# Loads of x moved to GpSimd's queue, products made four ahead, and preparation's transfers reordered

## The chip, the cores and the metric

The kernel runs on one core of a Trainium2 chip. The metric is device time in microseconds (us) of one execution. The engines are TensorE (PE in the profile), VectorE (DVE), ScalarE (ACT), GpSimd (POOL) and SyncE (SP); SyncE, ScalarE and GpSimd also issue transfers (DMA), and these issues are shown as SPq, ACTq and POOLq.

## The reference

The input is x of shape (1024, 39, 64): 1024 rows b, 39 fields f, 64 embedding columns e. Three layers of a compressed interaction network follow, each a product of the layer's state with the input, mixed by a weight matrix:

```
def _cin_layer(Xk, X0, W, b):
    Wr = W.reshape(O, Hk, Fdim)
    return jnp.einsum('bhe,bfe,ohf->boe', Xk, X0, Wr) + b[None, :, None]

Xk = X0
for W, b in ((W0, b0), (W1, b1), (W2, b2)):
    Xk = _cin_layer(Xk, X0, W, b)
    outs.append(Xk.sum(axis=-1))
return concatenate(outs, axis=-1) @ fc_w.T + fc_b
```

The output has one number per row b. All values are float32.

## The kernel before, in words

The sum over e and the final weights allow the last two layers to be folded. Preparation folds W2 and W1 with fc_w into one table (`wide`, in device memory) and lays W0 out in another (`wide0`). The main matmul then takes, for each column (b, e), the products of pairs of fields and gives 128 rows: 64 that stand for the folded upper layers and 64 of the first layer. Products of fields are symmetric, so all pairs of the 39 fields are covered by seven chunks of 117 = 3 x 39 products: each chunk multiplies two tiles in which the fields are rotated by different distances.

The 65536 columns (b, e) are worked in NBLK = 32 blocks of BLK = 2048 columns. For one block n:

- `load(n)` brings x into `xs`, 39 partitions of 2048 columns, in rows of 64 numbers (256 bytes).
- `store(n)` writes `xs` twice, one copy under the other, into a scratch tensor `xd` in device memory (78 rows of 8 KB).
- `roll(n)` reads four tiles `r0` to `r3` of 117 rows from `xd`, each with its own rotation (936 KB each), and two thirds of a fifth tile, `q`, whose last third holds ones.
- `product(n, c)`, c = 0 to 6, multiplies two of these tiles on VectorE into `p`. The pairs in order are r0 r1, r0 r2, r1 r2, r0 r3, r1 r3, r2 r3, r0 q.
- `multiply(n, c, p)` runs four matmuls of 512 columns with the weights `wa[:, c]` and adds into the block's two accumulators `po` (each of 1024 columns).
- `fields(n)` copies `xs` on ScalarE into the lower rows of two tiles `g`.
- `finish(n)` works the accumulators off: ScalarE adds a bias (`x1`), VectorE multiplies it with the other half into `g` and sums over e into `sums`, twice per block.

Loads, stores and rolls are all issued on SyncE's queue. In block n it issues roll(n+1), then load(n+2), then store(n+2), which waits for that load. Buffers: three of `xs`, four of `xd`, two each of r0 to r3 and q, four of `p`, four accumulators, two each of `g` and `x1`. The order within each engine is that of the code (`manual_schedule`). Transfers issue in order on each queue and wait for the tiles that they read or overwrite.

Before the loop, SyncE loads W2, then block 0 of x, stores it, loads block 1 and issues roll(0). ScalarE loads the small weights and W1, later writes ten pieces (`part`) of the folded table to `wide`. GpSimd copies W0 four times into `wide0` and gathers from it the right half of `wa` and `wb`, row by row (117 rows of 256 bytes per gather). The left halves are gathered from `wide`: those of `wa` by ScalarE, those of `wb` by SyncE (lines 213 to 219). In block 0 VectorE adds `wb[:, c]` to `wa[:, c]` (line 284) before the first matmul of chunk c.

The lines of the loop that set the order:

```
for n in range(NBLK):
    if n + 1 < NBLK:
        roll(n + 1)
    if n + 2 < NBLK:
        load(n + 2)
        store(n + 2)
    for c in range(NCHUNK):
        p = product(n, c)
        if n == 0:
            nc.vector.tensor_tensor(wa[:, c], wa[:, c], wb[:, c], ALU.add)
        multiply(n, c, p)
        if n > 0 and c == 3:
            finish(n - 1)
    fields(n)
```

Lines named below: load L106, store L112 and L113, rolls L118 (r) and L120, L121 (q), wide0 copies L135, part writes L194, gathers L201 and L204, product L237, matmul L244, field copy L256, bias L263, the two steps of finish on VectorE L267 and L271, the add of the weights L284.

Of the kernel before, what the change touches and what calls it, by code (L numbers as in the profile page):

```python
# [48 lines left out]
PAIRS = ((0, 1), (0, 2), (1, 2), (0, 3), (1, 3), (2, 3))  # L49
NCHUNK = len(PAIRS) + 1  # L50
MM = 512
SUB = 1024
BLK = 2048
# [3 lines left out]
FW = 2 * F  # L57
# [21 lines left out]
def cin_kernel(ctx: ExitStack, tc: tile.TileContext, x, w0t, b0, w1, b1, w2, b2, fc_w, fc_b, out):  # L79
# [10 lines left out]
    work = ctx.enter_context(tc.tile_pool(name="work", bufs=2))  # L90
# [4 lines left out]
    q = []  # L95
    for i in range(2):
        qt = const.tile([K, BLK], F32, name=f"q{i}")
        nc.gpsimd.memset(qt, 1.0)  # L98
        q.append(qt)

    xv = x.rearrange("b f e -> f b e")
    xs, xd, r = {}, {}, {}

    def load(n):
        xs[n] = stage.tile([F, BLK], F32, name="xs", tag="xs")
        nc.sync.dma_start(  # L106
            xs[n].rearrange("p (b e) -> p b e", e=E), xv[:, n * BB : (n + 1) * BB, :]
        )

    def store(n):  # L110
        xd[n] = xds.tile([FW, BLK], F32, name="xd", tag="xd")
        nc.sync.dma_start(xd[n][0:F], xs[n])  # L112
        nc.sync.dma_start(xd[n][F:FW], xs[n])  # L113

    def roll(n):
        r[n] = [rolls.tile([K, BLK], F32, name=f"r{i}", tag=f"r{i}") for i in range(4)]
        for i in range(4):
            nc.sync.dma_start(r[n][i], rows(xd[n], BASE[i], [(1, F), (STEP[i], NG)], BLK))  # L118
        qt = q[n % 2]
        nc.sync.dma_start(qt[0:K:NG], xd[n][LAST : LAST + F])  # L120
        nc.sync.dma_start(qt[1:K:NG], xd[n][0:F])  # L121


    w2s = const.tile([H, FH], F32, name="w2s")
    nc.sync.dma_start(w2s, w2)
    fc = const.tile([H, 3], F32, name="fc")
    nc.scalar.dma_start(fc, fc_w.rearrange("o (l h) -> h (o l)", h=H))
    w1s = const.tile([H, FH], F32, name="w1s")
    nc.scalar.dma_start(w1s, w1)
    wide0 = dram.tile([FW * FW, H], F32, name="wide0")  # L130
    wide0v = wide0.rearrange("(b a) h -> b (a h)", a=FW)
    w0v = w0t.rearrange("b a h -> b (a h)")
    for i in range(2):
        for k in range(2):
            nc.gpsimd.dma_start(  # L135
                wide0v[i * F : (i + 1) * F, k * F * H : (k + 1) * F * H], w0v
            )
    bias = const.tile([H, 2], F32, name="bias")
    nc.scalar.dma_start(bias[:, 0:1], b1.rearrange("(h o) -> h o", o=1))
    nc.scalar.dma_start(bias[:, 1:2], b2.rearrange("(h o) -> h o", o=1))  # L140
    b0s = const.tile([128, 1], F32, name="b0s")
    nc.scalar.dma_start(b0s[H:128], b0.rearrange("(h o) -> h o", o=1))
    fcb = const.tile([1, 1], F32, name="fcb")
    nc.scalar.dma_start(fcb, fc_b.rearrange("(p o) -> p o", o=1))

    load(0)
    store(0)
    load(1)
    roll(0)

    wa = const.tile([K, NCHUNK, 2 * H], F32, name="wa")
    wb = const.tile([K, NCHUNK, 2 * H], F32, name="wb")
    nc.vector.memset(wa[:, NCHUNK - 1, :], 0.0)
    nc.vector.memset(wb[:, NCHUNK - 1, :], 0.0)
    wfin = const.tile([H + F, 1], F32, name="wfin")
    nc.vector.memset(wfin[0:H], 1.0)
    fc2 = const.tile([H, 32], F32, name="fc2")
    nc.vector.tensor_copy(fc2, fc[:, 2:3].to_broadcast([H, 32]))  # L158

    v2 = const.tile([H, FX], F32, name="v2")  # L160
    nc.vector.tensor_copy(v2[:, FW:FX], fc[:, 1:2].to_broadcast([H, 2]))


    n8 = 8 * F
    pv = psum.tile([128, 2, MM], F32, name="pv", tag="po")
    for half in range(2):
        for t in range(4):
            g = 4 * half + t
            nc.tensor.matmul(  # L169
                pv[32 * t : 32 * t + 32, half, 0:n8],  # L170
                fc2,
                w2s[:, g * n8 : (g + 1) * n8],
                start=True,
                stop=True,
            )
    vrow = const.tile([128, 2, n8], F32, name="vrow")
    for half in range(2):
        nc.vector.tensor_copy(vrow[:, half], pv[:, half, 0:n8])  # L178
        nc.scalar.dma_start(v2[32 * half : 32 * half + 32, 0:F], vrow[0:128:32, half])
    nc.vector.tensor_copy(v2[:, F:FW], v2[:, 0:F])  # L180


    w1v = w1s.rearrange("o (h f) -> o f h", f=F)
    wide = dram.tile([FX * FW, H], F32, name="wide")
    widev = wide.rearrange("(b a) h -> b (a h)", a=FW)
    for g in range(5):
        f0, f1 = 8 * g, min(8 * g + 8, F)
        n = (f1 - f0) * H
        pt = psum.tile([128, SUB], F32, name="pt", tag="po")
        nc.tensor.matmul(pt[0:FX, :n], v2, w1v[:, f0:f1, :], start=True, stop=True)  # L190
        part = const.tile([FX, MM], F32, name=f"part{g}")
        nc.vector.tensor_copy(part[:, :n], pt[0:FX, :n])  # L192
        for k in range(2):
            nc.scalar.dma_start(widev[:, (k * F + f0) * H : (k * F + f1) * H], part[:, :n])  # L194


    def gather(engine, dst, table, i, k, cols):

        first = BASE[k] * FW + BASE[i]
        steps = [(FW + 1, F), (STEP[k] * FW + STEP[i], NG)]  # L200
        engine.dma_start(dst[:, cols], rows(table, first, steps, H))  # L201
# [4 lines left out]
    tcol, wcol = slice(0, H), slice(H, 2 * H)  # L206
    for c, (i, k) in enumerate(PAIRS):
        gather(nc.gpsimd, wa[:, c], wide0, i, k, wcol)
        gather(nc.gpsimd, wb[:, c], wide0, k, i, wcol)
    line(nc.gpsimd, wa, wide0, 0, wcol, LAST * FW, FW + 1)  # L210
    line(nc.gpsimd, wb, wide0, 0, wcol, LAST, FW + 1)
    line(nc.gpsimd, wa, wide0, 1, wcol, 0, FW + 1)
    for c, (i, k) in enumerate(PAIRS):
        gather(nc.scalar, wa[:, c], wide, i, k, tcol)
        gather(nc.sync, wb[:, c], wide, k, i, tcol)
    line(nc.scalar, wa, wide, 0, tcol, LAST * FW, FW + 1)
    line(nc.sync, wb, wide, 0, tcol, LAST, FW + 1)
    line(nc.scalar, wa, wide, 1, tcol, 0, FW + 1)
    line(nc.sync, wa, wide, 2, tcol, FW * FW, 1)
    store(1)  # L220


# [5 lines left out]
    kfin = const.tile([1, 1], F32, name="kfin")  # L228
    nc.scalar.activation(kfin, pc[0:1, MM : MM + 1], AF.Identity, bias=fcb, scale=float(E))

    sums = const.tile([H + F, B], F32, name="sums")
    po, g = {}, {}

    def product(n, c):
        a, b = (r[n][PAIRS[c][0]], r[n][PAIRS[c][1]]) if c < len(PAIRS) else (r[n][0], q[n % 2])
        p = prods.tile([K, BLK], F32, name="p", tag="p")
        nc.vector.tensor_tensor(p, a, b, ALU.mult)  # L237
        return p

    def multiply(n, c, p):  # L240
        if c == 0:
            po[n] = [psum.tile([128, SUB], F32, name="po", tag="po") for _ in range(BLK // SUB)]
        for m in range(BLK // MM):
            nc.tensor.matmul(  # L244
                po[n][m // 2][:, bass.ts(m % 2, MM)],
                wa[:, c, :],
                p[:, bass.ts(m, MM)],
                start=(c == 0),
                stop=(c == NCHUNK - 1),
            )  # L250
# [21 lines left out]
                sums[:, b_at : b_at + SB], gt.rearrange("p (b e) -> p b e", e=E), AX.X, ALU.add  # L272
            )

    for n in range(NBLK):
        if n + 1 < NBLK:
            roll(n + 1)
        if n + 2 < NBLK:
            load(n + 2)
            store(n + 2)  # L280
        for c in range(NCHUNK):
            p = product(n, c)
            if n == 0:
                nc.vector.tensor_tensor(wa[:, c], wa[:, c], wb[:, c], ALU.add)  # L284
            multiply(n, c, p)
            if n > 0 and c == 3:
                finish(n - 1)
        fields(n)
    finish(NBLK - 1)

    y = const.tile([1, B], F32, name="y")
# [47 lines left out]
```

## Time and profile before

| what | value |
|---|---|
| time, median of 3 runs | 911.06 us (905.61 to 913.46) |
| the profiled execution | 906.01 us, span 904.2 us |
| TensorE matmuls busy | 808.2 us, 89% of the span |
| VectorE busy | 659.8 us, 73% |
| ScalarE busy | 140.8 us, 16% |
| GpSimd busy | 15.0 us, 2% |
| granted TensorE clock, mean | 0.985 |
| moved by transfers | 179.36 MB, 198 GB/s |

The profile is of one execution. The span runs from the first to the last instruction; 1.8 us of the execution's time lie outside it. A row of a group gives line, engine, operation, tiles written and read, shapes, count, then busy us, mean ns of one, and the idle time of the engine before these instructions with what ended most of it. A row in order of time gives start, duration, engine and operation, and in brackets the idle time before it and what ended it. A row of waits gives the total in us, how often, and the longest. The busy time of matmuls is modelled from their pipelining.

### The profile page before, as it was taken

The numbers are of one execution on the slowest core, as the hardware profiler recorded it, in microseconds if no ns is written. First come the engines' busy times: TensorE is split into PE (matmuls) and PEld (weight loads), VectorE is DVE, ScalarE is ACT, GpSimd is POOL, SyncE is SP. The second block draws the span as 40 slices with busy tenths as digits, with TensorE's granted clock in tenths as the row PEclk, the third lists the DMA queues.
The fourth block names the chain that finished last, engine by engine and source line by source line (L and its number), as shares of the span: only waits on it lengthen the run. The fifth ranks groups of instructions, "written<-read, shape, count | busy, mean of one in ns | idle before, by whom it ended". The sixth has DMA issues, their size and how long they took to land.

```text
span 904.2 us, 4982 instructions
## 1 busy us (share of the span) xinstructions
PE 808.2 (89%) x1828; PEld 344.5 (38%) x1828; DVE 659.8 (73%) x372; ACT 140.8 (16%) x133; POOL 15.0 (2%) x25
## 2 busy tenths in 40 slices
PE   1369999989989998999999998999989988998996
PEld 0024444434434433444344443433433333333432
DVE  0258888768968776888777786885867865778855
ACT  0001111110111111011111111011111110111112
POOL 4100000000000000000000000000000000000000
PEclk9999999999999999999999999999999999998999
DMA  8666676766667766666567766667675676766640
GB/s 190 199 226 205 176 233 229 229 167 187 211 186 240 215 229 190 225 227 217 163 218 215 240 237 179 190 173 190 236 229 176 165 179 214 230 159 191 221 149 0
DMA packets 67819, 179.36 MB, mean 198 GB/s; under 512 B 46548, under 2 KB 46747, under 8 KB 47544
## 3 DMA queue, kind: packets, MB, share of 16 engines
q1 hardware_dynamic: 64614, 174.66, 63.6%
q10 hardware_dynamic: 2446, 2.45, 1.1%
q0 software_dynamic: 736, 1.95, 0.7%
q8 instruction: 14, 0.23, 0.1%
q14 instruction: 9, 0.07, 0.0%
HBM read 156.98 MB, written 23.61 MB: 200 GB/s over the span
## 4 chain that ended last, share of the span: by engine, by line
DMA 79%; SPq 14%; PE 2%; DVE 2%; issue 2%; ACT 0%; ACTq 0%; DVEq 0%
DMA xs<-in_x 54%; DMA xd<-xs 20%; SPq L118 8%; SPq L120 3%; SPq L121 2%; DMA r<-xd 2%; DMA v<-vrow 1%; SPq L112 1%; PE pt L190 1%; DMA q<-xd 1%; PE po L244 1%; DVE p L237 1%; DMA fc<-in_fc_w 1%; DMA wide<-part 1%; DVE g L267 1%
## 5 line engine op out<-in xcount | busy, mean ns | idle before, releaser
L244 PE MATMUL po<-p,wa 117*128 117x512 f32 x1792 | 794.0, 603 | 70.8 <-DVE p L237 47.0
L237 DVE TENSOR_TENSOR p<-r,r 117x2048 f32<-117x2048 f32 x192 | 431.7, 2286 | 195.5 <-DMA r<-xd 173.7
L244 PEld LDWEIGHTS po<-p,wa 117*128 117x128 f32 x1792 | 341.2, 193 | 522.8 <-issue 429.6
L263 ACT ACTIVATE x<-po,b0s 64x1024 f32<-64x1024 f32 x64 | 71.1, 1110 | 385.4 <-PE po L244 385.4
L256 ACT COPY g<-xs 39x1024 f32<-39x1024 f32 x64 | 66.7, 1043 | 328.1 <-DVE sums L271 328.1
L267 DVE SCALAR_TENSOR_TENSOR g<-po,fc,x 64x1024 f32<-64x1024 f32 x64 | 81.2, 1269 | 5.7 <-ACT x L263 5.7
L271 DVE TENSOR_REDUCE sums<-g 103x16 f32<-103x1024 f32 x64 | 78.1, 1220 | 2.2
L237 DVE TENSOR_TENSOR p<-r,q 117x2048 f32<-117x2048 f32 x32 | 73.1, 2283 | 0.8 <-issue 0.8
L190 PE MATMUL pt<-w1s,v 64*80 64x512 f32 (+1 forms) x10 | 9.5, 1109 | 11.5 <-DVE v L180 11.5
L284 DVE TENSOR_TENSOR wa<-wa,wb 117x128 f32<-117x128 f32 x7 | 2.0, 285 | 10.0 <-DMA wb<-wide 10.0
L190 PEld LDWEIGHTS pt<-w1s,v 64*80 64x80 f32 x10 | 2.2, 228 | 18.3 <-DVE v L180 12.6
L169 PE MATMUL pv<-w2s,fc 64*32 64x312 f32 x16 | 2.3, 724 | 6.9 <-DVE fc L158 6.9
L192 DVE COPY part<-pt 80x512 f32<-80x512 f32 (+1 forms) x5 | 3.4, 674 | 6.8 <-PE pt L190 6.8
L227 ACT ACT_TABLE_LOAD x1 | 1.3, 1283 | 43.7 <-DMA wa<-wide 43.7
L180 DVE COPY v<-v 64x39 f32<-64x39 f32 x1 | 0.2, 176 | 10.4 <-DMA v<-vrow 10.4
L294 PE MATMUL py<-sums,wfin 103*1 103x512 f32 x4 | 2.0, 590 | 3.7 <-DVE sums L271 3.7
L201 POOL DMA_DIRECT2D wb<-wide x6 | 4.5, 744 | 0.0
L201 POOL DMA_DIRECT2D wa<-wide x6 | 4.2, 704 | 11.7 <-DMA wide<-in_w0t 11.6
L158 DVE COPY fc<-fc 64x32 f32<-64x32 f32 x1 | 0.2, 173 | 5.5 <-DMA fc<-in_fc_w 5.5
L98 POOL MEMSET q<- 117x2048 f32 x2 | 3.5, 1804 | 0.3 <-POOLq L326 0.3
L169 PEld LDWEIGHTS pv<-w2s,fc 64*32 64x32 f32 x16 | 0.6, 154 | 7.6 <-DVE fc L158 6.9
L178 DVE COPY vrow<-pv 128x312 f32<-128x312 f32 x2 | 0.9, 476 | 2.4 <-PE pv L169 2.4
(21 smaller groups left out, 8.2 us busy)
## 6 DMA issues: line engine op xcount, KB each, us to landing
r<-xd SPq DMA_DIRECT2D x128, 936.0 KB
xd<-xs SPq DMA_DIRECT2D x64, 312.0 KB
q<-xd SPq DMA_DIRECT2D x64, 312.0 KB
xs<-in_x SPq DMA_DIRECT2D x32, 312.0 KB
wide<-in_w0t POOLq DMA_DIRECT2D x4, 380.2 KB, 10.2
wide<-part ACTq DMA_DIRECT2D x8, 160.0 KB
w2s<-in_w SPq DMA_DIRECT2D x1, 624.0 KB
w1s<-in_w ACTq DMA_DIRECT2D x1, 624.0 KB
```

The lines of the kernel that those rows point to most:

```text
L112: nc.sync.dma_start(xd[n][0:F], xs[n])
L118: nc.sync.dma_start(r[n][i], rows(xd[n], BASE[i], [(1, F), (STEP[i], NG)], BLK))
L120: nc.sync.dma_start(qt[0:K:NG], xd[n][LAST : LAST + F])
L121: nc.sync.dma_start(qt[1:K:NG], xd[n][0:F])
L190: nc.tensor.matmul(pt[0:FX, :n], v2, w1v[:, f0:f1, :], start=True, stop=True)
L201: engine.dma_start(dst[:, cols], rows(table, first, steps, H))
L237: nc.vector.tensor_tensor(p, a, b, ALU.mult)
L244: nc.tensor.matmul(po[n][m // 2][:, bass.ts(m % 2, MM)], wa[:, c, :], p[:, bass.ts(m, MM)], start=(c == 0), stop=(c == NCHUNK - 1),)
L256: nc.scalar.copy(gt[H : H + F], xs[n][:, bass.ts(h, SUB)])
L263: nc.scalar.activation(t, po[n][h][H:128, :], AF.Identity, bias=b0s[H:128])
L267: nc.vector.scalar_tensor_tensor(gt[0:H], po[n][h][0:H, :], fc[:, 0:1], x1[h], ALU.add, ALU.mult)
L271: nc.vector.tensor_reduce(sums[:, b_at : b_at + SB], gt.rearrange("p (b e) -> p b e", e=E), AX.X, ALU.add)
```

## The change

The loads of blocks 1 and up are issued on GpSimd's queue, three blocks ahead of the block that TensorE works on; `xs` gets four buffers and `xd` five. The order on SyncE in block n is roll(n+1), store(n+2). Products are made four chunks ahead of the matmuls that use them, across the block's border; the finish of the block before, and the copies of fields, follow the first chunk's matmuls instead of the fourth's and the seventh's. In preparation two of the four `wide0` copies go from GpSimd to ScalarE, block 1 of x is loaded on GpSimd after its gathers together with block 2, q is filled with ones later on GpSimd, and the first four `wb` gathers from `wide` go from SyncE to ScalarE, each behind the `wa` gather of its chunk. Tiles that only preparation uses lie in a pool of their own, whose space `g` and `x1` take over. No arithmetic is changed.

The diff, cut to its core:

```diff
-    xds = ctx.enter_context(tc.tile_pool(name="xds", bufs=4, space=DRAM))
-    stage = ctx.enter_context(tc.tile_pool(name="stage", bufs=3))
+    xds = ctx.enter_context(tc.tile_pool(name="xds", bufs=5, space=DRAM))
+    stage = ctx.enter_context(tc.tile_pool(name="stage", bufs=4))
...
-    def load(n):
+    def load(n, engine):
         xs[n] = stage.tile([F, BLK], F32, name="xs", tag="xs")
-        nc.sync.dma_start(
+        engine.dma_start(
...
+        nc.sync.dma_start(w2s, w2)
+        nc.scalar.dma_start(fc, fc_w.rearrange("o (l h) -> h (o l)", h=H))
+        nc.scalar.dma_start(w1s, w1)
+        load(0, nc.sync)
+        for i in range(2):
+            for k in range(2):
+                engine = nc.scalar if i else nc.gpsimd
+                engine.dma_start(wide0v[i * F : (i + 1) * F, k * F * H : (k + 1) * F * H], w0v)
...
-    load(0)
-    store(0)
-    load(1)
-    roll(0)
+        store(0)
+        roll(0)
...
-    for c, (i, k) in enumerate(PAIRS):
-        gather(nc.scalar, wa[:, c], wide, i, k, tcol)
-        gather(nc.sync, wb[:, c], wide, k, i, tcol)
...
+    def gathers(engine, other, table, cols):
+        for c, (i, k) in enumerate(PAIRS):
+            gather(engine, wa[:, c], table, i, k, cols)
+            gather(engine if c < 4 else other, wb[:, c], table, k, i, cols)
+        line(engine, wa, table, 0, cols, LAST * FW, FW + 1)
+        line(other, wb, table, 0, cols, LAST, FW + 1)
+        line(engine, wa, table, 1, cols, 0, FW + 1)
+
+    gathers(nc.gpsimd, nc.gpsimd, wide0, slice(H, 2 * H))
+    load(1, nc.gpsimd)
+    load(2, nc.gpsimd)
+    gathers(nc.scalar, nc.sync, wide, slice(0, H))
+    line(nc.sync, wa, wide, 2, slice(0, H), FW * FW, 1)
     store(1)
...
+    AHEAD = 4
+    steps = [(n, c) for n in range(NBLK) for c in range(NCHUNK)]
+    p = {s: product(*s) for s in steps[:AHEAD]}
+    for at, (n, c) in enumerate(steps):
+        if c == 0:
+            if n + 1 < NBLK:
+                roll(n + 1)
+            if n + 2 < NBLK:
+                store(n + 2)
+            if n + 3 < NBLK:
+                load(n + 3, nc.gpsimd)
+        if n == 0:
+            nc.vector.tensor_tensor(wa[:, c], wa[:, c], wb[:, c], ALU.add)
+        multiply(n, c, p.pop((n, c)))
+        if c == 0:
+            if n > 0:
+                finish(n - 1)
+            fields(n)
+        if at + AHEAD < len(steps):
+            p[steps[at + AHEAD]] = product(*steps[at + AHEAD])
     finish(NBLK - 1)
```

More of the change, by code (lines that the diff above doesn't have):

```diff
@@ L130, in cin_kernel @@
+    bias = const.tile([H, 2], F32, name="bias")
+    b0s = const.tile([128, 1], F32, name="b0s")
+    fcb = const.tile([1, 1], F32, name="fcb")
+    wfin = const.tile([H + F, 1], F32, name="wfin")
+    kfin = const.tile([1, 1], F32, name="kfin")
+    q = [const.tile([K, BLK], F32, name=f"q{i}") for i in range(2)]
     wide0 = dram.tile([FW * FW, H], F32, name="wide0")
     wide0v = wide0.rearrange("(b a) h -> b (a h)", a=FW)
[L132 to L137, printed above, removed]
@@ L152, in cin_kernel @@
[L152 to L165, printed above, removed]
@@ L166, in cin_kernel @@
[L166 to L179, printed above, removed]
@@ L180, in cin_kernel @@
-    nc.vector.tensor_copy(v2[:, F:FW], v2[:, 0:F])
-    w1v = w1s.rearrange("o (h f) -> o f h", f=F)
     wide = dram.tile([FX * FW, H], F32, name="wide")
     widev = wide.rearrange("(b a) h -> b (a h)", a=FW)
[L186 to L194, printed above, removed]
+    prep = tc.tile_pool(name="prep", bufs=1)
@@ new lines, in cin_kernel @@
+    with prep as prep:
+        w2s = prep.tile([H, FH], F32, name="w2s")
+        w1s = prep.tile([H, FH], F32, name="w1s")
+        nc.sync.dma_start(w2s, w2)
+        nc.scalar.dma_start(fc, fc_w.rearrange("o (l h) -> h (o l)", h=H))
+        nc.scalar.dma_start(w1s, w1)
+        load(0, nc.sync)
+        w0v = w0t.rearrange("b a h -> b (a h)")
+        for i in range(2):
+            for k in range(2):
+                engine = nc.scalar if i else nc.gpsimd
+                engine.dma_start(wide0v[i * F : (i + 1) * F, k * F * H : (k + 1) * F * H], w0v)
+        nc.scalar.dma_start(bias[:, 0:1], b1.rearrange("(h o) -> h o", o=1))
+        nc.scalar.dma_start(bias[:, 1:2], b2.rearrange("(h o) -> h o", o=1))
+        nc.scalar.dma_start(b0s[H:128], b0.rearrange("(h o) -> h o", o=1))
+        nc.scalar.dma_start(fcb, fc_b.rearrange("(p o) -> p o", o=1))
+        for qt in q:
+            nc.gpsimd.memset(qt, 1.0)
+        store(0)
+        roll(0)
+        nc.vector.memset(wa[:, NCHUNK - 1, :], 0.0)
+        nc.vector.memset(wb[:, NCHUNK - 1, :], 0.0)
+        nc.vector.memset(wfin[0:H], 1.0)
+        nc.vector.tensor_copy(fc2, fc[:, 2:3].to_broadcast([H, 32]))
+        nc.vector.tensor_copy(v2[:, FW:FX], fc[:, 1:2].to_broadcast([H, 2]))
+        n8 = 8 * F
+        pv = psum.tile([128, 2, MM], F32, name="pv", tag="po")
+        vrow = prep.tile([128, 2, n8], F32, name="vrow")
+        for half in range(2):
+            for t in range(4):
+                g = 4 * half + t
+                nc.tensor.matmul(
+                    pv[32 * t : 32 * t + 32, half, 0:n8],
+                    fc2,
+                    w2s[:, g * n8 : (g + 1) * n8],
+                    start=True,
+                    stop=True,
+                )
+            nc.vector.tensor_copy(vrow[:, half], pv[:, half, 0:n8])
+            nc.scalar.dma_start(v2[32 * half : 32 * half + 32, 0:F], vrow[0:128:32, half])
+        nc.vector.tensor_copy(v2[:, F:FW], v2[:, 0:F])
+        w1v = w1s.rearrange("o (h f) -> o f h", f=F)
+        for g in range(5):
+            f0, f1 = 8 * g, min(8 * g + 8, F)
+            n = (f1 - f0) * H
+            pt = psum.tile([128, SUB], F32, name="pt", tag="po")
+            nc.tensor.matmul(pt[0:FX, :n], v2, w1v[:, f0:f1, :], start=True, stop=True)
+            part = prep.tile([FX, MM], F32, name=f"part{g}")
+            nc.vector.tensor_copy(part[:, :n], pt[0:FX, :n])
+            for k in range(2):
+                nc.scalar.dma_start(widev[:, (k * F + f0) * H : (k * F + f1) * H], part[:, :n])
@@ L273, in finish @@
             )
[L275 to L286, printed above, removed]
+    AHEAD = 4
[14 more added lines that the diff above has]
+            if n > 0:
                 finish(n - 1)
-        fields(n)
+            fields(n)
+        if at + AHEAD < len(steps):
+            p[steps[at + AHEAD]] = product(*steps[at + AHEAD])
     finish(NBLK - 1)
```

36 lines of the change are left out of this document (5 added, 31 removed).

## The prediction

> **What bounds the kernel now.** I read the page's first and fourth parts, then SyncE's waits, then one block of the loop in order of time. Busy shares first, as us, share of the span, instructions:
>
> ```profile
> PE 808.2 (89%) x1828; PEld 344.5 (38%) x1828; DVE 659.8 (73%) x372; ACT 140.8 (16%) x133; POOL 15.0 (2%) x25
> DMA xs<-in_x 54%; DMA xd<-xs 20%; SPq L118 8%; SPq L120 3%; SPq L121 2%; DMA r<-xd 2%; DMA v<-vrow 1%; SPq L112 1%; PE pt L190 1%; DMA q<-xd 1%; PE po L244 1%; DVE p L237 1%; DMA fc<-in_fc_w 1%; DMA wide<-part 1%; DVE g L267 1%
> SPq L112 <- DMA xs<-in_x: 480.0, 31, 19.3
> SPq L118 <- DMA xd<-xs: 134.6, 62, 3.8
> ```
>
> TensorE is busy for 89%, yet the chain that ended last runs through transfers and SyncE's queue: 54% is the landing of a load, 20% that of a store. SyncE itself waits for the load 31 times, 480.0 us (15.5 each). One block of SyncE's work, with the first and the last rolls of the loop around it, start and duration in us:
>
> ```profile
> 59.06 4.12 SPq L118 DMA_DIRECT2D r<-xd  x4
> ...
> 470.24 0.30 SPq L112 DMA_DIRECT2D xd<-xs  x1
> ...
> 475.10 3.88 SPq L118 DMA_DIRECT2D r<-xd  x4
> ...
> 480.59 0.56 SPq L106 DMA_DIRECT2D xs<-in_x  x1
> 496.77 0.31 SPq L112 DMA_DIRECT2D xd<-xs  x1
> ...
> 853.90 4.03 SPq L118 DMA_DIRECT2D r<-xd  x4
> ```
>
> Rolls, then the load (5.5 us later), its landing and the store (16.2 later), the store's landing and the next rolls (470.24 to 475.10: 4.86). Together 26.5 us. Over the span, 30 such periods lie between the rolls at 59.06 and those at 853.90: 26.49 us each. This ring is the bound. TensorE's own need is less:
>
> ```profile
> 58.90 0.19 PEld L244 LDWEIGHTS po<-p,wa 117*128 117x128 f32 x1 [0.24 <-issue]
> ...
> 74.78 0.19 PEld L244 LDWEIGHTS po<-p,wa 117*128 117x128 f32 x1 [0.24 <-issue]
> L244 PE MATMUL po<-p,wa 117*128 117x512 f32 x1792 | 794.0, 603 | 70.8 <-DVE p L237 47.0
> ```
>
> 37 matmul steps lie between the two weight loads, so one step is 0.429 us; a block has 1792/32 = 56, so 24.04 us, and 32 blocks 769.2 us. The row of all matmuls shows 794.0 busy (24.8 more) and 47.0 of waits for products.
>
> **The change, part by part.** *The load leaves SyncE's queue.* Its four-line ring loses the load and its wait; what remains is rolls, store, landing, rolls. What the transfers themselves need is read from windows of 2 us (length, busy PE, PEld, DVE, ACT, POOL, granted clock, transfer share, GB/s):
>
> ```profile
> 490.00:492.00 2.00, 2.00 (x6) 0.81 (x5) 2.00 (x2) 0.00 (x0) 0.00 (x0) 1.00 0.86 266
> 492.00:494.00 2.00, 2.00 (x6) 0.93 (x5) 2.00 (x2) 0.00 (x0) 0.00 (x0) 1.00 0.91 159
> 494.00:496.00 2.00, 2.00 (x6) 0.80 (x6) 2.00 (x2) 0.00 (x0) 0.00 (x0) 1.00 0.68 61
> 496.00:498.00 2.00, 2.00 (x6) 0.92 (x5) 1.97 (x3) 0.42 (x1) 0.00 (x0) 1.00 0.31 75
> ```
>
> The rate falls at about 492.5, where the roll's big rows end and the load's 256-byte rows begin: the rolls took 17.4 us from their issue, the load another 4.3 (to 496.77) at a high share for few bytes. The store now issues behind the rolls without waiting, so its issue and start are covered; I put 3.6 of its 4.86 us behind the rolls (estimate: the wait for landing, at most 3.8 in the row above). The transfer ring is then 17.4 + 3.6 = 21.0 us if the load runs wholly in gaps, 25.3 if it costs its 4.3 in full. With the store's latency uncovered too it is 17.4 + 4.86 + 4.3 = 26.5, nothing gained. I take half of the load, 23.1, since share 0.31 in the window at 496 shows a gap of a few us in each period but not one that fits the load whole. That is under TensorE's 24.04: **the bound passes to TensorE.**
>
> Does VectorE keep up?
>
> ```profile
> L237 DVE TENSOR_TENSOR p<-r,r 117x2048 f32<-117x2048 f32 x192 | 431.7, 2286 | 195.5 <-DMA r<-xd 173.7
> L267 DVE SCALAR_TENSOR_TENSOR g<-po,fc,x 64x1024 f32<-64x1024 f32 x64 | 81.2, 1269 | 5.7 <-ACT x L263 5.7
> L271 DVE TENSOR_REDUCE sums<-g 103x16 f32<-103x1024 f32 x64 | 78.1, 1220 | 2.2
> 484.86 2.29 DVE L237 TENSOR_TENSOR p<-r,r 117x2048 f32<-117x2048 f32 x1 [3.76 <-DMA r<-xd]
> 488.37 2.29 DVE L237 TENSOR_TENSOR p<-r,r 117x2048 f32<-117x2048 f32 x1 [1.22 <-DMA r<-xd]
> ```
>
> A block asks 7 x 2.286 + 2 x 1.269 + 2 x 1.220 = 21.0 us of it, under 24.04.
>
> *Products four ahead; finish after the first chunk.* No work is added. Product s+4 waits for the matmuls of chunk s (four buffers). Queued behind it on VectorE at a block's start T: the product for chunk 3 (to T+2.3), the finish of the block before (5.0, to T+7.3), the product for chunk 4 (to T+9.6), which TensorE wants at T+4x3.43 = T+13.7. So 4 us of cover; if the finish were late by more, TensorE would wait. The last product of a block ends at about T+14.2, and only then may the rolls two blocks on overwrite its tiles. They have 24 x 2 - 14 = 34 us until TensorE wants them; the first product starts 9.8 after the issue (475.10 to 484.86), the second 13.3 after, so 12 us suffice. The 47.0 us of product waits should nearly go; I keep 5 for rolls that run late (the longest load wait, 19.3 against 15.5, shows that transfers vary by some 4 us).
>
> *The slow clock.* Of the 24.8 us over 769.2, five steps at the start go at half pace (0.85 us from one weight load to the next), 5 x 0.43 = 2.2; the others come at and after waits, where the granted clock falls:
>
> ```profile
> 55.18 0.34 PEld L244 LDWEIGHTS po<-p,wa 117*128 117x128 f32 x1 [0.52 <-issue]
> 56.03 0.34 PEld L244 LDWEIGHTS po<-p,wa 117*128 117x128 f32 x1 [0.52 <-issue]
> ...
> 81.00:109.00 28.00, 28.00 (x66) 12.35 (x65) 24.42 (x14) 4.97 (x5) 0.00 (x0) 1.00 0.67 192
> 800.00:870.00 70.00, 65.31 (x145) 28.20 (x144) 50.37 (x27) 11.88 (x11) 0.00 (x0) 0.95 0.68 212
> ```
>
> Clock 1.00 where TensorE never pauses, 0.95 where it does. Without the waits I count this as gone, all but the 2.2.
>
> *Preparation reordered.* Now TensorE starts at 54.16:
>
> ```profile
> 18.00 0.33 SPq L106 DMA_DIRECT2D xs<-in_x  x1
> 28.59 14.87 SPq L118 DMA_DIRECT2D r<-xd  x4
> 36.83 0.89 ACTq L201
> 37.75 4.07 DMA wa<-wide
> 44.35 9.18 DMA q<-xd
> 45.19 7.08 SPq L201 DMA_DIRECT2D wb<-wide  x6
> 53.82 0.29 DVE L284 TENSOR_TENSOR wa<-wa,wb 117x128 f32<-117x128 f32 x1 [10.03 <-DMA wb<-wide]
> 54.16 21.20 PE L244 MATMUL po<-p,wa 117*128 117x512 f32 x44 [23.52 <-DMA wb<-wide]
> ```
>
> The last to come is the first wb gather: on SyncE behind the rolls, issued at 45.19 and landed by 53.82. It moves to ScalarE as the second gather, 36.83 + 0.89 + 0.89 + 4.07 = 42.7. But four products now precede the add on VectorE, so all four r tiles must have landed first. Lower bound of the start: 43. Upper: the fourth r landed before q (44.35 + 9.18 = 53.5), plus a product and the add: 56. The rolls' issue stretched over 14.87 us here and 3.88 in the loop, so waits on other transfers held them; if these stay, the start stays near the upper end. The first load of block 1 no longer stands ahead of the rolls (18.00), but two copies of wide0 join ScalarE's queue, and three loads, the two moved copies and the parts' writes share the transfers with the rolls. I take 47.5, nearer the gathers, whose row ended the wait. SyncE keeps 4 of its 8 gather issues, some 6 us less, so the rolls of block 1 go at 53 instead of 59; TensorE wants them at 47.5 + 2.2 + 24.0 = 73.7, 53 + 12 = 65 is in time.
>
> *GpSimd.* It now issues a load per block, and nothing waits behind it there.
>
> ```profile
> L201 POOL DMA_DIRECT2D wa<-wide x6 | 4.2, 704 | 11.7 <-DMA wide<-in_w0t 11.6
> ...
> 22.96 0.69 DVE L192 COPY part<-pt 80x512 f32<-80x512 f32 x1 [2.25 <-PE pt L190]
> 23.13 0.59 POOL L201 DMA_DIRECT2D wa<-wide  x1
> ```
>
> A gather of 117 rows takes it 0.70 us; a load has 39 x 32 = 1248 rows, at most 1248/117 x 0.70 = 7.5 us (estimate, if it goes by rows), at least 0.7. Under 24.04 and three blocks early, it costs nothing. The load into a fourth buffer waits for ScalarE's copies of the block four before, long done.
>
> **The sum**, against the profiled execution (906.01 us, span 904.2, 1.8 around it): start 47.5, first slow matmuls 2.2, 32 blocks 769.2, waits left 5, tail as now 8.7 (TensorE starts at 54.16 after 23.5 of its 70.8 idle, so it ends at 54.16 + 794.0 + 47.3 = 895.5). Span 832.6, time **834**. The profiled run lies 0.6% under the median 911.06; I predict on its level.
>
> **Rivals.** *Transfers stay the bound, at a shorter period.* For it: their share already stands at 0.86 while rolls run, and the change moves no byte less. The Trainium skill, "DMA: Bandwidth & Descriptors", section "Issuing engines are not separate DMA queues", says so of any such move: transfers of all issuing engines share the same 16 engines, and another queue saves issue time alone. The windows agree that the load keeps the engines busy (0.91 and 0.68 in its 4 us). Against it: gaps exist (0.31). Price: rolls of block 1 at 53, 30 periods, and 50.3 from the last rolls to the end (853.90 to 904.2), plus 1.8. At 25.0 us 855, at 26.0 885. It decides above 24.04.
>
> *Nothing gained in the loop*: load additive and latency uncovered, 26.5 us; 53 + 795 + 50.3 + 1.8 = 900, the start alone.
>
> *Slower: GpSimd writes the load's rows only while VectorE rests.* VectorE is busy 21.0 us per block; if GpSimd's 7.5 fit only beside that, the period is 28.5, and the time 53 + 855 + 50.3 + 1.8 = 960. It decides once the building takes over 5.5 us and is shut out. Against it: the gather issued at 23.13, in the middle of a copy on VectorE (22.96 to 23.65), took 0.59 us, less than the mean 0.70. The Trainium skill, "SBUF — State Buffer", section "Who interferes with whom", has VectorE's copies in a two-port mode shut GpSimd out, but by inference not a product of two tensors; no run here shows it for products.
>
> **How the numbers follow.** Forecast 0.62; transfers bound 0.22; nothing gained 0.08; slower 0.05; the rest 0.03 for a late start that adds to any. Range: low 820 (start 43 and no waits make 825; 5 more if the reordering brings the parts' landing forward), high 885 (transfers at 26.0). Two in ten lie outside. A measurement here tells about 1% from no change: faster 0.88, within 1% 0.07 (nearly all of the third case, which lies 0.7% under the profiled time), slower 0.05.
>
> **What would show it.** Right: SyncE's longest wait is no longer a load; rolls come every 24.0 us; the product waits fall from 47.0 to about 5; granted clock 1.00 throughout; the matmul row near 775 busy; first matmul at 43 to 56. Wrong: product waits on r still in the hundreds on VectorE and rolls 25 us or more apart (transfers), or GpSimd's load issues of many us with SyncE waiting for xs (rival three).

## The result, and the profile after

The changed kernel took **858.88 us** (median of 4 runs, 856.32 to 861.70), beside 912.26 us for the kernel before in the same series. The ratio is 0.9415, with a 95% interval of 0.9339 to 0.9492: 5.8% faster. The forecast was 834 in a range of 820 to 885. So the time lies inside the range, and 25 us above the forecast. Every ratio in this document is to the kernel before in its own series of runs, and counts only the runs within 1.5% of the fastest of their kernel.

The page of the changed kernel, the same parts as shown of before: busy shares, the chain by line, the row of all main matmuls, the products, GpSimd's loads, and SyncE's longest wait.

```profile
PE 794.1 (93%) x1828; PEld 346.0 (40%) x1828; DVE 664.1 (77%) x372; ACT 140.9 (16%) x133; POOL 44.0 (5%) x54
...
PE po L239 89%; DMA wide<-part 2%; DMA xs<-in_x 2%; DMA r<-xd 1%; DMA v<-vrow 1%; DMA xd<-xs 1%; ACTq L197 1%; DMA wa<-wide 0%; DVE g L262 0%; DVE sums L266 0%; PE pt L186 0%; PE py L295 0%; SPq L200 0%; DVE wa L282 0%; DMA q<-xd 0%
...
L239 PE MATMUL po<-p,wa 117*128 117x512 f32 x1792 | 778.8, 597 | 34.6 <-DVE wa L282 34.6
L232 DVE TENSOR_TENSOR p<-r,r 117x2048 f32<-117x2048 f32 x192 | 436.8, 2289 | 142.9 <-PE po L239 132.3
...
L98 POOL DMA_DIRECT2D xs<-in_x x31 | 30.1, 975 | 680.3 <-DMA xd<-xs 397.6
...
SPq L110 <- DMA xd<-xs: 437.6, 35, 18.7
```

The busy shares hardly moved (TensorE from 89% to 93%), but the chain changed altogether: 89% of it is now the main matmul (L239; L244 before), where 74% were a load's and a store's landing. Products now wait for TensorE (132.3 of 142.9 us) and hardly for rolls (173.7 before). SyncE's longest wait is for a store's landing and no longer for a load's. The loop as SyncE's rolls in order of time:

```profile
452.72 3.43 SPq L110 DMA_DIRECT2D r<-xd  x4
476.75 3.43 SPq L110 DMA_DIRECT2D r<-xd  x4
500.79 3.76 SPq L110 DMA_DIRECT2D r<-xd  x4
```

And as two long windows (length, busy PE, PEld, DVE, ACT, POOL, granted clock, transfer share, GB/s):

```profile
200.00:500.00 300.00, 300.00 (x700) 132.81 (x699) 258.00 (x140) 53.81 (x50) 12.58 (x13) 1.00 0.65 228
500.00:800.00 300.00, 300.00 (x700) 132.81 (x699) 254.66 (x137) 53.35 (x50) 9.67 (x10) 1.00 0.66 225
```

A period is 24.03 us (26.49 before), and for 600 us TensorE does not pause once, at a granted clock of 1.00. What is left to explain is therefore outside the loop. The 34.6 us that TensorE waited are all put down to the add of the weights, VectorE's L282 (L284 before), which exists in block 0 alone. Block 0 in order of time, from the fourth product to the third burst, and the last:

```profile
50.48 2.29 DVE L232 TENSOR_TENSOR p<-r,r 117x2048 f32<-117x2048 f32 x1 [4.07 <-DMA r<-xd]
52.69 0.28 DVE L282 TENSOR_TENSOR wa<-wa,wb 117x128 f32<-117x128 f32 x1
53.03 6.84 PE L239 MATMUL po<-p,wa 117*128 117x512 f32 x8 [19.04 <-DVE wa L282]
59.91 2.29 DVE L232 TENSOR_TENSOR p<-r,r 117x2048 f32<-117x2048 f32 x1 [6.93 <-PE po L239]
62.12 0.28 DVE L282 TENSOR_TENSOR wa<-wa,wb 117x128 f32<-117x128 f32 x1
62.46 5.40 PE L239 MATMUL po<-p,wa 117*128 117x512 f32 x8 [2.59 <-DVE wa L282]
67.89 2.29 DVE L232 TENSOR_TENSOR p<-r,r 117x2048 f32<-117x2048 f32 x1 [5.49 <-PE po L239]
70.10 0.28 DVE L282 TENSOR_TENSOR wa<-wa,wb 117x128 f32<-117x128 f32 x1
70.44 3.70 PE L239 MATMUL po<-p,wa 117*128 117x512 f32 x8 [2.59 <-DVE wa L282]
...
97.15 5.27 PE L239 MATMUL po<-p,wa 117*128 117x512 f32 x8 [2.58 <-DVE wa L282]
```

VectorE's order is product 4, add 1, product 5, add 2, and so on. Product 4 needs the buffer that the matmuls of chunk 0 read, so it starts when they end (59.91), and the add for chunk 1, which needs nothing but landed weights, stands behind it. TensorE waits for that add. So each of chunks 1 to 6 in block 0 is strictly serial: matmuls, product, add, matmuls. That is six waits of 2.6 us, 15.6 in all. The first burst takes 6.84 us and the six others 3.70 to 5.40, instead of 8 x 0.429 = 3.43. Two of these as windows, the slow steps of the second burst and the whole of the third:

```profile
62.40:66.40 4.00, 3.94 (x5) 1.65 (x6) 0.00 (x0) 0.00 (x0) 0.00 (x0) 0.57 0.77 168
70.40:74.10 3.70, 3.66 (x8) 1.44 (x8) 0.00 (x0) 0.00 (x0) 0.00 (x0) 1.00 0.84 261
```

In three of the six bursts behind a pause the first steps go at half pace, at a granted clock of 0.52 to 0.57; the other three keep 1.00. The first burst goes at half pace throughout, though its window (53.03 to 59.90) shows 1.00.

Against the profiled execution (858.69 us, span 856.9) the terms of the forecast's sum are: start 53.03 for 47.5 (+5.5), waits 15.6 for 5 (+10.6), matmuls busy 778.8 for 771.4 (+7.4), tail 9.5 for 8.7 (+0.8). Together +24.3, and 832.6 + 24.3 = 856.9.

### The profile page after: what moved, and what is told of

The parts are those of the page before. It is cut to its first block, busy times and chain, and to the rows that moved or that the text cites. A ratio compares the mean times of both kernels' runs of the same rounds, so it can differ in the third digit from the quotient of the medians.

```text
span 856.9 us, 5040 instructions
## 1 busy us (share of the span) xinstructions
PE 794.1 (93%) x1828; PEld 346.0 (40%) x1828; DVE 664.1 (77%) x372; ACT 140.9 (16%) x133; POOL 44.0 (5%) x54
## 3 DMA queue, kind: packets, MB, share of 16 engines
q0 software_dynamic: 4080, 11.11, 5.8%
## 4 chain that ended last, share of the span: by engine, by line
PE 89%; DMA 7%; issue 1%; DVE 1%; ACTq 1%; SPq 0%; ACT 0%; DVEq 0%
PE po L239 89%; DMA wide<-part 2%; DMA xs<-in_x 2%; DMA r<-xd 1%; DMA v<-vrow 1%; DMA xd<-xs 1%; ACTq L197 1%; DMA wa<-wide 0%; DVE g L262 0%; DVE sums L266 0%; PE pt L186 0%; PE py L295 0%; SPq L200 0%; DVE wa L282 0%; DMA q<-xd 0%
## 5 line engine op out<-in xcount | busy, mean ns | idle before, releaser
L239 PE MATMUL po<-p,wa 117*128 117x512 f32 x1792 | 778.8, 597 | 34.6 <-DVE wa L282 34.6
L232 DVE TENSOR_TENSOR p<-r,r 117x2048 f32<-117x2048 f32 x192 | 436.8, 2289 | 142.9 <-PE po L239 132.3
L239 PEld LDWEIGHTS po<-p,wa 117*128 117x128 f32 x1792 | 342.9, 192 | 469.9 <-issue 422.4
L98 POOL DMA_DIRECT2D xs<-in_x x31 | 30.1, 975 | 680.3 <-DMA xd<-xs 397.6
```

The lines of the kernel that those rows point to most:

```text
L98: engine.dma_start(xs[n].rearrange("p (b e) -> p b e", e=E), xv[:, n * BB : (n + 1) * BB, :])
L239: nc.tensor.matmul(po[n][m // 2][:, bass.ts(m % 2, MM)], wa[:, c, :], p[:, bass.ts(m, MM)], start=(c == 0), stop=(c == NCHUNK - 1),)
```

## The experiments

The theory: the time between 834 and 859 went into block 0, through the place of the adds in the written order, and into the start. The rivals: rolls or loads that run late, GpSimd's queue, and preparation's order.

**The add ahead of the product.** In block 0 only, the add for chunk c+1 is moved in front of product c+4, behind which it stood.

```diff
     p = {s: product(*s) for s in steps[:AHEAD]}
+    nc.vector.tensor_tensor(wa[:, 0], wa[:, 0], wb[:, 0], ALU.add)
...
-        if n == 0:
-            nc.vector.tensor_tensor(wa[:, c], wa[:, c], wb[:, c], ALU.add)
         multiply(n, c, p.pop((n, c)))
+        if n == 0 and c + 1 < NCHUNK:
+            nc.vector.tensor_tensor(wa[:, c + 1], wa[:, c + 1], wb[:, c + 1], ALU.add)
```

> Undoes one thing in block 0 alone: VectorE adds the weights of chunk c+1 ahead of the product for chunk c+4 instead of behind it. Theory (the in-order queue: in the changed kernel that product waits for the matmuls of chunk c, so the add, and with it chunk c+1, cannot start before them): the six waits of 2.6 us in block 0 (15.6 in all) vanish and about 6 us of half-pace matmuls with them; first matmul still near 53; the loop stays at 24.0 per block; time about 837. Rival (block 0 is late because gathers and rolls land late): the waits stay under another name, time 853 or more.

Measured: 843.98 us (843.31 to 845.39), ratio 0.9278 [0.9211, 0.9345], 14.9 us under the changed kernel. Its row of matmuls:

```profile
L239 PE MATMUL po<-p,wa 117*128 117x512 f32 x1792 | 774.0, 595 | 24.5 <-DVE wa L273 18.1 <-DVE wa L284 6.4
```

The place of the one wait behind the start, in order of time:

```profile
75.14 2.29 DVE L232 TENSOR_TENSOR p<-r,r 117x2048 f32<-117x2048 f32 x1 [8.13 <-DMA r<-xd]
77.34 0.28 DVE L284 TENSOR_TENSOR wa<-wa,wb 117x128 f32<-117x128 f32 x1
77.69 2.93 PE L239 MATMUL po<-p,wa 117*128 117x512 f32 x3 [6.40 <-DVE wa L284]
```

The six waits of 2.6 are gone. Of the 7 us above the expected 837, 6.4 are one new wait, again an add behind a product: the add for chunk 5 stands behind the first product of block 1, and that waits 8.13 us for block 1's rolls. The theory holds, and the same mechanism struck again one step further.

**The old loop order, all else as changed.** Products are written as before, one per chunk, the finish behind the fourth chunk.

```diff
-    p = {s: product(*s) for s in steps[:AHEAD]}
-    for at, (n, c) in enumerate(steps):
...
+        for c in range(NCHUNK):
+            p = product(n, c)
+            if n == 0:
+                nc.vector.tensor_tensor(wa[:, c], wa[:, c], wb[:, c], ALU.add)
+            multiply(n, c, p)
+            if n > 0 and c == 3:
+                finish(n - 1)
+        fields(n)
```

> The changed kernel with the old order of statements in the loop: each product right before its matmuls, finish after the fourth chunk, field copies last; loads on GpSimd three blocks ahead as changed. Theory (four product buffers had let VectorE run four ahead all along, so the written lead changes nothing but block 0, where it puts products ahead of the adds): loop 24.0, no product waits, block 0 without its six waits, time about 837, faster than the changed kernel. Rival (the lead covers late products): waits for products in every block, time 865 or more.

Measured: 836.51 us (834.54 to 837.76), ratio 0.9186 [0.9105, 0.9268], span 836.0. The row of all matmuls:

```profile
L239 PE MATMUL po<-p,wa 117*128 117x512 f32 x1792 | 772.8, 594 | 19.5 <-DVE wa L280 17.2 <-DVE p L232 2.3
```

And the first ones in order of time:

```profile
51.83 26.98 PE L239 MATMUL po<-p,wa 117*128 117x512 f32 x56 [17.18 <-DVE wa L280]
```

Block 0 is one unbroken run of 56 matmuls. Of the 34.6 us of waits only the start's 17.2 and 2.3 at products remain. **The written lead costs 22.4 us and gains nothing in the loop**: without it, too, TensorE is busy for all of the 600 us from 200 to 800. With four product buffers VectorE already runs up to four products ahead of TensorE wherever the tiles are there; its order from block 1 on is the same in both forms (four products, the finish, three products). The lead changed only where the adds stand.

**The loads back on SyncE, two ahead, as before.**

```diff
-    load(2, nc.gpsimd)
...
             if n + 2 < NBLK:
+                load(n + 2, nc.sync)
                 store(n + 2)
-            if n + 3 < NBLK:
-                load(n + 3, nc.gpsimd)
```

> The changed kernel with the loads of blocks 2 and up back on SyncE, two blocks ahead, between rolls and store, as before the change; all else as changed. Theory (the ring of load, store and rolls is the whole gain of the loop): rolls again every 26.5 us, time about 905 to 915, no faster than before. Rival (making products ahead covers late rolls): period 25.5 or less, time under 885.

Measured: 900.0 us (median of 10 runs, 887.69 to 910.90), ratio 0.9831 [0.9762, 0.9901]; the five runs that the ratio counts have a median of 894.52. That is under the 905 to 915 of the theory and over the 885 of the rival. The profiled execution took 908.99, 1.6% above those, so its sizes are rough. Its longest wait on SyncE:

```profile
SPq L104 <- DMA xs<-in_x: 490.0, 31, 19.5
```

Its row of matmuls:

```profile
L238 PE MATMUL po<-p,wa 117*128 117x512 f32 x1792 | 798.5, 606 | 65.6 <-DVE p L231 33.8 <-DVE wa L280 31.5
```

The ring of before is back: 31 waits for the load, 490.0 us (480.0 before), the rolls of blocks 1 to 31 every 26.68 us (57.90 to 858.27), and product waits of 33.8. So the move of the loads, with the distance, is where most of the gain comes from: 36 us (894.52 less 858.88) of 53.

**Three ahead, but on SyncE's queue.** The kernel with the old loop order, with one word changed: the load three ahead stands on SyncE's queue behind the store. The lines are against that kernel.

```diff
         if n + 3 < NBLK:
-            load(n + 3, nc.gpsimd)
+            load(n + 3, nc.sync)
```

> The kernel of e4 with the loads, still three blocks ahead, issued on SyncE behind the store of the block. Theory (the ring is broken because nothing waits for a load that was issued a block earlier; the queue it goes through does not matter while the transfers need less than TensorE's 24.0): loop 24.0, time within 1% of e4, 832 to 842. Rival (a load behind the rolls on the same queue still holds the next rolls up): period 25 or more, time 860 or more.

Measured: **834.15 us** (832.79 to 834.38), ratio 0.9291 [0.9238, 0.9344], span 832.2: under both kernels, and level with the form on GpSimd's queue (836.51 in another series). The row of matmuls:

```profile
L239 PE MATMUL po<-p,wa 117*128 117x512 f32 x1792 | 772.1, 594 | 16.1 <-DVE wa L280 16.1
```

SyncE's longest wait and a window of the loop:

```profile
SPq L110 <- DMA xd<-xs: 403.4, 35, 16.0
```

```profile
200.00:500.00 300.00, 300.00 (x701) 132.96 (x700) 258.03 (x140) 53.79 (x50) 0.00 (x0) 1.00 0.65 226
```

Not one product wait is left, and TensorE is busy for all of the window as with GpSimd. GpSimd's queue was not needed; what counted was that a store no longer waits for a load issued just before it, on the queue that must issue the next rolls. By the Trainium skill, "DMA: Bandwidth & Descriptors", section "Issuing engines are not separate DMA queues", the other queue saves issue time alone; for the time of the whole kernel the trace agrees (834.15 and 836.51).

**Old preparation, new loop.** The diff of preparation is undone and the loop kept, with the loads of blocks 1 and 2 placed to suit.

```diff
+    load(0, nc.sync)
+    store(0)
+    load(1, nc.sync)
+    roll(0)
...
+    line(nc.gpsimd, wa, wide0, 1, wcol, 0, FW + 1)
+    load(2, nc.gpsimd)
```

> The changed loop behind the preparation of the kernel before (loads 0 and 1 on SyncE, all four wide0 copies on GpSimd, wb gathers on SyncE); load 2 is on GpSimd behind its gathers. Theory (the preparation's reordering moved the first matmul by a microsecond, 54.16 to 53.03): first matmul 54 to 57, loop 24.0, time 859 to 863, the same within 1%. Rival (the reordering carries a good part of the gain): time 870 or more.

Measured: 870.18 us (867.39 to 873.50), ratio 0.9565 [0.9487, 0.9643]: at the rival's 870, and 7 us over the theory's 863. The end of preparation in order of time:

```profile
51.14 7.35 SPq L201 DMA_DIRECT2D wb<-wide  x6
63.00 0.29 DVE L288 TENSOR_TENSOR wa<-wa,wb 117x128 f32<-117x128 f32 x1 [2.10 <-DMA wb<-wide]
63.34 1.22 PE L245 MATMUL po<-p,wa 117*128 117x512 f32 x1 [32.15 <-DVE wa L288]
```

The first matmul comes at 63.34 instead of 53.03, since the wb gathers stand on SyncE behind the rolls and go out only at 51.14. The new order of preparation is worth 11 us in this company.

**What the transfers alone need.** Two kernels with chunks 2 to 5 left out of every block, so that neither TensorE nor VectorE sets the pace, one with the load on GpSimd, one with it on SyncE behind the store; each was run a second time.

```diff
-        for c in range(NCHUNK):
+        for c in (0, 1, NCHUNK - 1):
             p = product(n, c)
...
-            if n > 0 and c == 3:
+            if n > 0 and c == 1:
                 finish(n - 1)
```

> The kernel of e4 with chunks 2 to 5 left out of the loop (their products and matmuls, so the result lacks them); all transfers are kept. TensorE then needs 10.3 us per block and VectorE 11.9, so the rolls' period is that of the transfers alone with the loads on GpSimd. The prediction took 23.1 between 21.0 (load wholly in gaps) and 25.3 (load in full). Theory: 22 to 24. Rival (the transfers have no room): 24.0 or more, so that TensorE's bound in the changed kernel was a near thing.

> As e6_bare_gpsimd (chunks 2 to 5 left out), with the loads three ahead on SyncE behind the store. If transfers of all queues share the same engines and the queue only saves issue time: the same period as e6 within 0.7 us. If the load's small rows run better between the rolls' large ones from another queue: 1 us or more longer than e6.

> The bare kernel (chunks 2 to 5 of every block left out) with the load on GpSimd's queue once more. If its 22.20 us per period were a property of the kernel it comes again, 21.9 to 22.5; if it was the spread of one execution it may come near 20.7.

> The bare kernel (chunks 2 to 5 of every block left out) with the load on SyncE behind the store once more. If its 20.68 us per period is a property of the kernel it comes again, 20.4 to 21.0; if the difference was spread it may come near 22.2.

The rolls of block 1 and of block 31, then SyncE's wait for the store, with the load on GpSimd's queue:

```profile
63.39 4.55 SPq L110 DMA_DIRECT2D r<-xd  x4
...
729.52 3.43 SPq L110 DMA_DIRECT2D r<-xd  x4
```

```profile
SPq L110 <- DMA xd<-xs: 488.8, 39, 21.5
```

The same two views with the load on SyncE:

```profile
61.81 4.05 SPq L110 DMA_DIRECT2D r<-xd  x4
...
682.31 3.43 SPq L110 DMA_DIRECT2D r<-xd  x4
```

```profile
SPq L110 <- DMA xd<-xs: 414.6, 38, 17.5
```

Thirty periods: 666.13 / 30 = 22.20 us on GpSimd's queue and 620.50 / 30 = 20.68 on SyncE's. The repeats gave 22.14 (63.03 to 727.24) and 20.49 (60.96 to 675.65); the times were 765.32 and 767.13 us against 723.87 and 718.41. So the transfer ring lies under TensorE's 24.04 on either queue, by 1.8 and 3.4 us, and the difference of 1.5 came again in a second execution of each, so it belongs to the kernels. I had expected none over 0.7. By the rule of the Trainium skill's page and section just named, another queue changes nothing but the issue time; here the form on GpSimd's queue took 7% longer per period (22.20 against 20.68), and the measurement decides.

To see whether the load's place or its queue costs this, the load was put on SyncE in front of the store:

```diff
-        if n + 2 < NBLK:
-            store(n + 2)
         if n + 3 < NBLK:
             load(n + 3, nc.sync)
+        if n + 2 < NBLK:
+            store(n + 2)
```

> Leaves out chunks 2 to 5 of every block, as the two bare kernels before it, so that TensorE and VectorE rest most of each period; the load three ahead stands on SyncE's queue, now in front of the store instead of behind it. Read: the period between rolls from block 1 to block 31 (22.20 with the load on GpSimd's queue, 20.68 with it on SyncE behind the store). Theory place: what lengthens the period on GpSimd's queue is that the load takes bandwidth between the store's issue and its landing, for which the next rolls wait; in front of the store it must do the same, 21.7 to 22.7 us per period. Rival queue: it is GpSimd's queue itself (its larger packets, its own share of the engines) that costs, and then SyncE's load costs the same in either place, 20.4 to 21.0. Rival burst: only the spread between executions, then the two repeated kernels beside it will not keep their difference.

Its rolls of block 1 went at 61.32 and those of block 31 at 699.87: 21.29 us per period, 740.1 us, between the two and in neither's interval. In the bare kernels on GpSimd's queue the load too was issued ahead of the store (at 400.96 and 403.18 us in one period), so place and queue may share the 1.5 us; that is argued from one run and not shown. In front of the store on SyncE the load has one more effect, which a period of that run shows:

```profile
403.23 0.54 SPq L98 DMA_DIRECT2D xs<-in_x  x1
403.81 7.98 SPq L104 DMA_DIRECT2D xd<-xs  x1
411.84 0.37 SPq L105 DMA_DIRECT2D xd<-xs  x1
```

The issue of the store behind the load holds SyncE for 7.98 us (8.07 in the median of all), where it takes 0.54 in the other bare kernels. What the queue's part consists of, and why the issue is held, stays open. The pages' rows of transfers (packets and bytes; and for GpSimd's queue packets, MB, share) differ in one more thing, GpSimd's queue first:

```profile
DMA packets 32168, 179.27 MB, mean 235 GB/s; under 512 B 8487, under 2 KB 8686, under 8 KB 11901
...
q0 software_dynamic: 4080, 11.11, 5.8%
```

And SyncE's:

```profile
DMA packets 65488, 179.22 MB, mean 248 GB/s; under 512 B 44070, under 2 KB 44269, under 8 KB 45222
...
q0 software_dynamic: 832, 1.81, 1.0%
```

The two differ in the queue of 29 loads: from GpSimd's queue a load goes in 112 packets ((4080 - 832) / 29), on SyncE's about one for each of its 1248 rows of 256 bytes. The form with fewer and larger packets was not the faster one here.

**The first rolls on GpSimd.** With the old loop order, roll(0) was issued from GpSimd behind its gathers, to take it off SyncE, where the wait for the parts holds it.

```diff
-        roll(0)
...
     gathers(nc.gpsimd, nc.gpsimd, wide0, slice(H, 2 * H))
+    roll(0, nc.gpsimd)
     load(1, nc.gpsimd)
```

> The kernel of e4 with the six transfers of block 0's rolls issued on GpSimd behind its gathers instead of on SyncE. Theory (in the changed kernel SyncE's rolls and ScalarE's part writes take turns waiting for each other's landings, which stretches the part writes to 15 us and the rolls to 24): part writes issue in about 8 us, the first ScalarE gather near 38 instead of 46, first matmul 43 to 47 instead of 51.8, time 829 to 833. Rival (the part writes and gathers wait for bandwidth that all share): first matmul 50 or later, time as e4 within 3 us.

Measured: 844.23 us (843.13 to 844.60), ratio 0.9408 [0.9337, 0.9479]; first matmul at 59.75, 8 us later rather than earlier. That is the rival's late start; the time misses both, the rival's by 5 us. Two windows of its preparation:

```profile
30.00:40.00 10.00, 4.17 (x11) 1.02 (x9) 2.35 (x4) 0.00 (x0) 3.44 (x4) 1.00 0.99 273
40.00:50.00 10.00, 0.00 (x0) 0.00 (x0) 1.94 (x1) 0.00 (x0) 0.00 (x0) 1.00 1.02 297
```

A step of its chain of work:

```profile
36.61 19.37 DMA wide<-part
```

The transfer share is full for 20 us, and a write of a part of the folded table, for which the gathers wait, takes 19.37 us to land among the rolls' megabytes. The ten part writes were issued in 9.71 us instead of 14.11, nearly as expected, and yet the first of ScalarE's gathers went at 56.08 instead of 46.27. The theory that issue held the start fell.

**The parts' writes on two queues.** On the form with the loads three ahead on SyncE: five of the ten writes go from GpSimd, whose own gathers come first.

```diff
+        gathers(nc.gpsimd, nc.gpsimd, wide0, slice(H, 2 * H))
         w1v = w1s.rearrange("o (h f) -> o f h", f=F)
...
             for k in range(2):
-                nc.scalar.dma_start(widev[:, (k * F + f0) * H : (k * F + f1) * H], part[:, :n])
...
+                engine = nc.gpsimd if k else nc.scalar
+                engine.dma_start(widev[:, (k * F + f0) * H : (k * F + f1) * H], part[:, :n])
...
-    gathers(nc.gpsimd, nc.gpsimd, wide0, slice(H, 2 * H))
```

> The kernel with the old loop order and the load on SyncE's queue three ahead, with one further change in the preparation: the ten writes of the weight parts go five to ScalarE's queue and five to GpSimd's, whose own gathers stand in front of them. Theory: ScalarE's queue alone took 12.85 us to issue the ten (27.68 to 40.5), while the parts come 1.9 us apart; on two queues they are out by about 36, ScalarE's first gather begins at about 40 instead of 44.25, the first matmul at about 47 instead of 50.69, and the time is 829 to 832 against 834.15. Rival: as with the first rolls on GpSimd's queue, earlier issues only meet the rolls' transfers, which fill the bandwidth until 42; the first gather stays at 43 to 46 and the time at 833 to 836.

Measured: 834.58 us (834.03 to 836.48), ratio 0.9189 [0.9126, 0.9253]: no gain over 834.15. The issues on ScalarE in order of time:

```profile
26.82 7.58 ACTq L209 DMA_DIRECT2D wide<-part  x5
```

Two steps of the chain:

```profile
34.09 11.46 DMA wide<-part
...
45.80 0.87 ACTq L137
```

The writes are issued by 35 instead of 40.5, yet the last lands at 45.55 and the first gather goes at 45.80 (44.25 in the form with one queue). The first matmul came at 49.49, 1.2 us earlier, not at the expected 47. As with the rolls on GpSimd, the first gather waits for landing, not for issue.

## Why the prediction was right, and where it was not

**The bound passes to TensorE: right.** Rolls 24.03 us apart against 24.04, TensorE without a pause, and the store's landing, not the load's, is now SyncE's longest wait, which costs nothing. The ring of the transfers was taken as 23.1 (21.0 to 25.3); with the pace of the other engines taken away it measures 22.20 and 22.14. Half of the load's 4.3 us was a fair choice, a little too much in the sum; its parts were not measured one by one. The first rival needed over 24.04, and lost by 1.8 us; in the experiment with the loads two ahead the period does grow again, to 26.68. The time alone would not have told: 858.88 lies near the 855 of that rival, and the rolls 24.03 us apart rule it out.

**VectorE keeps up: right.** 258.00 of 300 us busy is 20.7 per block (21.0 forecast), and the finish behind the first chunk's matmuls made TensorE wait nowhere.

**The waits left, 5 us: the step that failed.** The 5 were kept for rolls that run late in the loop, and there were none. In their place stand the 15.6 us of block 0. The prediction said of the products four ahead that "no work is added" and asked what is queued behind product s+4; it listed the finish and the next product, which is the list for block 1 and up. It noticed the adds only where four products precede the first one. In block 0 each add stands behind a product that waits for a buffer, and TensorE behind the add. Asking the same question of block 0 would have given it: 6 x (2.29 + 0.28) = 15.4, against 15.6 measured.

**The slow clock gone but for 2.2 us: wrong for the same reason.** The clock does stay at 1.00 where TensorE never pauses. But behind three of the six pauses it is down again, as a window of 28 us in block 0 and beyond shows, the one shown of before (there TensorE was busy for all of it at 1.00):

```profile
81.00:109.00 28.00, 20.24 (x43) 8.35 (x42) 13.95 (x11) 3.27 (x3) 0.00 (x0) 0.94 0.59 218
```

The term was 9.6 (778.8 less 769.2), not 2.2; 3.4 of it are the first burst (6.84 less 3.43). Where the adds do not interrupt block 0, it is 3.6 (772.8) and 2.9 (772.1).

**The start, 47.5: mis-sized, inside its bounds of 43 to 56.** It came at 53.03. The forecast leaned to the gathers, by their issue at 36.83 before. In the changed kernel both paths came late. ScalarE's first gather goes at 46.26 (36.83 before), and on the chain the part writes, which it needs, land up to 45.00. That they land late because the loads, the copies and the rolls now share the transfers with them is argued from the last two experiments, not shown. And the fourth r tile came at 50.48, with its product and the add right behind it, which is the path of the forecast's upper bound. Without the four products in front, the add still waited for a gather, and the first matmul came at 51.83, 1.2 us earlier. The rolls of block 1 went at 62.73, not at 53, since SyncE's own gathers could go only at 53.59, behind the rolls of block 0. That was still in time in the changed kernel, whose block 0 is slow; it cost the 6.40 us where the adds were moved (rolls at 61.99).

**GpSimd: right.** A load's issue takes it 0.975 us (bounds 0.7 to 7.5), with VectorE busy for 86% of the loop. It is not shut out while products run; this one lies within the product of 59.91 to 62.20 shown above:

```profile
61.04 0.97 POOL L98 DMA_DIRECT2D xs<-in_x  x1 [28.34 <-DMA xd<-xs]
```

The Trainium skill, "SBUF — State Buffer", section "Who interferes with whom", tells of a probe in which a copy on VectorE stalled transfers and a product of two tensors did not, and infers the reason; the trace agrees (0.975 us).

That the kernels with the old loop order come out at 834 to 837, the forecast's number, is partly chance: their start is 3 to 4 us later and their waits 3 to 5 us less than in its sum.

## What to carry to other kernels

On a queue that works in order, do not place a transfer that waits in front of one that does not need to: issuing the load one block earlier, behind the store, gave all of the gain in the loop, on the same queue. Before writing out a lead by hand, count the buffers: with four of them and an order that lets the engine run on, the lead is already there. And follow a new order through the first block by itself, since what stands there only once (here seven small adds) can come to stand behind a wait.

## What was not expected of the hardware

The same load issued from GpSimd's queue made the bare transfer ring 22.2 us, from SyncE's behind the store 20.6, though it went in 112 packets instead of some 1248; in front of the store on SyncE it was 21.3, and there the store's issue took 8.07 us instead of 0.54. And in preparation writes that were issued sooner did not land sooner: with transfers at a share of 0.99 and 1.02 a part's write took 19.37 us to land, and five writes moved to a second queue left the time at 834.58 against 834.15.
